# Cross-attention on one NeuronCore: the value products of two head groups run back to back, and the normalized input moves into three shared buffers

## The chip, the cores and the metric

The kernel runs on one core of one Trainium2 chip. The metric is the device time in microseconds. A core has a matrix engine (TensorE: PE for its matmuls, PEld for its weight loads), a vector engine (VectorE, DVE), a scalar engine (ScalarE, ACT), a general one (GpSimd, POOL) and a queue engine (SyncE, SP) that issues nearly every DMA of this kernel. Each engine works through its own instructions in the order in which the program gives them; engines wait for each other by semaphores.

## The reference

Layer normalization, a query projection, attention of 32 heads over a context that serves as keys and values, an output projection and a residual:

```python
x = (hidden - mu) * rsqrt(var + 1e-5) * gamma + beta   # hidden: 8 x 256 x 1024
Q = split_heads(x @ Wq.T)                              # 32 heads of 32
K = V = split_heads(ctx)                               # ctx: 8 x 256 x 1024
probs = softmax(where(mask, Q @ K.T / sqrt(32), -inf))
out = hidden + merge_heads(probs @ V) @ Wout.T         # all float32
```

## The kernel before

**The quad and the slot.** Four heads are 128 columns and make a quad; each of the 8 batches has 8 quads, so there are 64 quads, numbered n. The main loop at L938 has 64 passes; this text calls pass n "slot n". i is n modulo 8, and b in the loop is the batch whose output is projected in that slot (batch n // 8 - 1).

**What a slot puts on PE, in this order** (L963 to L1028): the scores of quad n + 1 (L486, 16 matmuls in the trace), the values of quad n - 2, which is probabilities times V (L636, 64 small matmuls on 64 rows by 32 columns, eight of them side by side in the array), "place 1" steps of the output projection (L720), one of the seven products of a later batch's query projection (L447), and "place 2" steps of the output projection. Both projections are done by Strassen's scheme in Winograd's form, seven half-size products A11, A12, S2, S3, A22, S1, S4 of four steps each; a step shows as two matmuls of 512 columns in the trace. `STEPS` (L669) says how many steps stand in each place of the slots i = 0 to 8 (8 is the next batch's slot 0); `PRODUCTS` gives their order. `ENDS` is the table of the last but one batch. The query product p of a batch falls into slot i = 2 + p.

**The accumulator of the output projection.** Pool `ps_o` has one buffer. The first step of A12, of S2 and of S1 begins a new sum in it, and so PE must wait there until DVE has read the sum before: `store(b, 0, 0)` in slot i = 2 (L762, before S2), `store(b, 1, 0)` in slot i = 6 (before S1), `store(b, 0, 1)` in slot i = 0. A11 has the query projection's buffer `ps_q`, which ACT empties in `keep_p1` (L728).

**What a slot puts on the other engines: `softmax(n + 1)`.** For each of the four heads j: DVE reads the two score tiles, adds the mask and finds the smallest value of the negated scores (L524), ACT takes the exponential and its sum (L528), DVE the reciprocal (L535), POOL multiplies (L543), DVE transposes 32 x 32 blocks into the tile `pT` (L549), and ACT copies a part aside (L555). In between ACT copies the finished values out of PSUM (`copy_at`, L649), DVE takes sums of the output projection (the "hooks") and a query product (`copies`). The next scores need the score buffers that L524 has read. At the end of the slot comes `tail` (L609): SP issues two DMAs that exchange quarters of `pT` (L614), then the loads of the list `between` (L615), then two more for `pT` (L618), each of which waits for its partner of L614 to land.

**The loads.** `between` holds, in this order, the V of the next two quads (odd slots) or a K (even slots), in some slots a half of `ring`, the weights of a query product (slots i = 7 and i = 0 hold the two halves of T1, 512 KB each), a residual (i = 0 to 3), and a half of the x of a later batch (L129, 512 KB).

**The path of x.** For batch b the tables at L816 to L842 give the slot of each step, relative to first = 8 (b - 1) + 2, the slot of its first query product. The two halves s = 0, 1 of x are loaded; DVE takes their statistics (`ln_stats`, L227 to L232, which stand behind the slot's softmax and ahead of the next slot's); ACT normalizes (L248); DVE transposes blocks into a second tile xe (`blocks_x`, L316); 16 DMAs move its blocks into a third tile xnT (`move_x`, L332), from which PE reads. x and xe alternate in two buffers of pool `xp`; xnT has two buffers of pool `lnp`, the first of which held batch 0's xnT.

```python
    loads=(first - 12, first - 11) if b == SPLIT + 1 else (first - 13, first - 12),
    stats=(first - 10, first - 8) if b == SPLIT + 1 else (first - 11, first - 9),
```

For b = 4 to 7 these are, by i: loads 5 and 6, statistics 7 and 1, moves 4, 5 and 6 (of the slots before the batch's first product).

Of the kernel before, what the change touches and what calls it, by code (L numbers as in the profile page):

```python
# [46 lines left out]
F32 = mybir.dt.float32  # L47
# [4 lines left out]
P = 128  # L52
# [7 lines left out]
def xattn_kernel(  # L60
# [15 lines left out]
    NQ = NC  # L76
# [9 lines left out]
    N = B * NQ  # L86

    const = ctx.enter_context(tc.tile_pool(name="const", bufs=1))
    xp = ctx.enter_context(tc.tile_pool(name="xp", bufs=2))
    rp = ctx.enter_context(tc.tile_pool(name="rp", bufs=4))  # L90
    lnp = ctx.enter_context(tc.tile_pool(name="lnp", bufs=2))
    kp = ctx.enter_context(tc.tile_pool(name="kp", bufs=2))
    vp = ctx.enter_context(tc.tile_pool(name="vp", bufs=2))
    atp = ctx.enter_context(tc.tile_pool(name="atp", bufs=3))
# [24 lines left out]
        nc.tensor.transpose(busy, ident, ident)  # L119


    xs, ks, vs, rs = {}, {}, {}, {}

    def load_x(b, s, h=None):

        if b not in xs:
            xs[b] = xp.tile([P, NS, D], F32, tag="x", name=f"x_{b}")
        cols = ds(0, D) if h is None else ts(h, 512)
        nc.sync.dma_start(xs[b][:, s, cols], x[b, ts(s, P), cols])  # L129

# [124 lines left out]
            ALU.subtract, ALU.mult,  # L255
        )

    xnT0 = lnp.tile([P, NC, S + 1], F32, tag="xnT", name="xnT_0")
    xnTs[0] = lambda c: xnT0[:, c, :]
    px0 = {}  # L260

# [36 lines left out]
    def transpose_x1(p):  # L298

        if p == 0:  # L300
            tile_ = lnp.tile([P, NC * (S + 1)], F32, tag="xnT", name="xnT_1")
            px1["to"] = tile_[:, : NC * S].rearrange("p (c t) -> p c t", c=NC)
# [9 lines left out]
    def blocks_x(b, s):  # L312

        if s == 0:
            xes[b] = xp.tile([P, NA, NC, NS, K], F32, tag="x", name=f"xe_{b}")
        nc.vector.transpose(  # L316
            xes[b][:, :, :, s, :],
            xs[b][:, s, :].rearrange("p (c q k) -> p q c k", c=NC, q=NA),
        )

    def move_x(b, part):

        if 0 in part:
            tile_ = lnp.tile([P, NC * (S + 1)], F32, tag="xnT", name=f"xnT_{b}")
            xnT = tile_[:, : NC * S].rearrange(
                "p (a c s k) -> p a c s k", a=NA, c=NC, s=NS
            )
# [167 lines left out]
    tails = []  # L495
    BY_ACT = range(1, 2 * NQ)
    BY_DVE = range(NQ, 2 * NQ)


    def softmax_parts(n, copies=(), ahead=(), between=(), hooks={}, fill=()):  # L500
# [9 lines left out]
                fill.pop(0)()  # L510

        pss = scs[n]
        pT = pTs[n] = ptp.tile([P, 2, NI, NH, NS, K], F32, tag="pT", name=f"pT_{n}")
        pc = asp.tile([P, NI, NH, NS, K], F32, tag="pc", name=f"pc_{n}")
        es, mns, dens = {}, {}, {}

# [40 lines left out]
        if n == 0:  # L557
            for j in range(NH - 1):
                exps(j, (0,))
            yield  # L560
            exps(NH - 1, (0,))
            fill_in()
            yield
            for j in range(NH):
                exps(j, (1,))
            normalize(0)
            fill_in()
        else:
            exps(0)
            while tails:  # L570
                tails.pop()()
            for done in list(pvs):
                copy_at(done)
            exps(1)
            for hook in hooks.get("soon", ()):
                hook()
            exps(2)
            normalize(0)
            exps(3)
        if n <= NQ + 1:  # L580
# [44 lines left out]
            tail()  # L625
        yield

    def values(n):
        pvs[n] = [
            ps_v.tile([P, 2, NS, K], F32, tag="pv", name=f"pv_{n}_{r}") for r in range(2)  # L630
        ]
        pT = pTs.pop(n)
        for i in range(NI):
            for j in range(NH):
                for r in range(2):
                    nc.tensor.matmul(  # L636
                        pvs[n][r][j * HD : (j + 1) * HD],
                        vs[n - n % 2][ts(r, 2 * K), i, ds(n % 2 * P + j * HD, HD)],
                        pT[ts(r, 2 * K), :, i, j, :, :],
                        start=(i == 0), stop=(i == NI - 1),  # L640
                    )

    def copy_at(n):
        b, c = divmod(n, NQ)
        k, c = divmod(c, NK)
        if c == 0:
            ats[b, k] = atp.tile([P, NK, NS, NA, K], F32, tag="at", name=f"at_{b}_{k}")
        for r, pv in enumerate(pvs.pop(n)):
            nc.scalar.copy(  # L649
                ats[b, k][:, c, :, ts(r, 2), :], pv.rearrange("p a s k -> p s a k")  # L650
            )
# [28 lines left out]

# [51 lines left out]

    def copy_po(b, i):
        if "tile" not in ends_kept:
            tile_ = lnp.tile([P, NC * (S + 1)], F32, tag="xnT", name="ends")
            ends_kept["tile"] = tile_[:, : 4 * 512].rearrange("p (i q) -> p i q", i=4)
        ends_kept[i] = ends_kept["tile"][:, i % 4]
        nc.scalar.copy(ends_kept[i], pos[b])

# [198 lines left out]
    for n in range(N):  # L938
# [17 lines left out]
        if n in (2, 4):  # L956
            between.append(partial(load_wo, B21, n // 2 - 1))
        if n == N - 4:
            again = xp.tile([P, NS, D], F32, tag="x", name="x_again")
# [203 lines left out]
```

## Time and profile before

| | |
|---|---|
| Time, median of 3 runs (lowest to highest) | 567.86 us (567.67 to 568.67) |
| Span of the profiled execution, first to last instruction | 566.0 us |
| Median time less that span | 1.9 us |
| Granted TensorE clock, mean | 1.000 |
| Busy share of PE, DVE, ACT, POOL | 99%, 83%, 75%, 70% |
| DMA | 119.02 MB in 47219 packets, mean 210 GB/s |

The profile is of one execution; the time of that execution itself is known by its span. The span runs from the first to the last instruction of the program, and the time has 1.9 us more than that around it. In the chain of waits every piece begins where the instruction of that piece is started and ends where the next piece begins, so the pieces of one engine add up without overlap. In the lists of instructions by time, a row is a run of one kind: its start, its length until the last one ends, and its count.

### The profile page before, as it was taken

To read this page: it belongs to the slowest core of one execution; us is meant where nothing else is said; L and a number is where in the kernel's file an instruction comes from. 1 tells how busy PE (TensorE), PEld (TensorE's weight loads), DVE (VectorE), ACT (ScalarE), POOL (GpSimd) and SP (SyncE) were. 2 spreads that over 40 slices of the span, in tenths; PEclk is the share of its full clock that TensorE was granted. 3 is DMA by queue.
4 is the path that set the end of the run, shared out by engine and by line. 5 is a ranking of instruction groups with operands and counts; after the bars stand their busy time and mean duration, and the time that the engine had idled before them with its cause. 6 is when DMAs were issued, how large, how long until landed. Compare 5 with 4: busy or idle time off the path is not lost.

```text
span 566.0 us, 20200 instructions
## 1 busy us (share of the span) xinstructions
PE 561.4 (99%) x7266; PEld 393.7 (70%) x7266; DVE 467.6 (83%) x1716; ACT 423.4 (75%) x1464; POOL 394.3 (70%) x636
## 2 busy tenths in 40 slices
PE   8999999999999999999999999999999999999997
PEld 8788886767766767667766776667766767755454
DVE  5889889999988988878898888988888777879923
ACT  4699999997778866786777876778776776769820
POOL 2788887899777656857568665777648657448780
PEclk9999999999999999999999999999999999999999
DMA  8966667856697777966778767796658864536751
GB/s 310 397 181 199 185 198 228 281 162 179 212 301 232 223 202 235 263 195 191 233 216 239 215 176 221 230 273 193 176 140 269 255 191 128 146 110 180 218 156 74
DMA packets 47219, 119.02 MB, mean 210 GB/s; under 512 B 8976, under 2 KB 9744, under 8 KB 47120
## 3 DMA queue, kind: packets, MB, share of 16 engines
q1 hardware_dynamic: 46976, 117.74, 69.5%
q8 instruction: 57, 0.93, 0.8%
q14 instruction: 42, 0.34, 0.2%
q10 hardware_dynamic: 144, 0.01, 0.0%
HBM read 66.33 MB, written 11.53 MB: 138 GB/s over the span
## 4 chain that ended last, share of the span: by engine, by line
PE 97%; DMA 1%; DVE 0%; POOL 0%; ACT 0%; issue 0%; SPq 0%; POOLq 0%
PE po_S L720 21%; PE pq_A L447 19%; PE pv L636 12%; PE sc L486 12%; PE po_A L720 11%; PE pq L345 9%; PE pq_S L447 8%; PE po_end L787 3%; PE po_last L787 1%; DMA x<-in_x_dram 1%; PE po_end_s L787 0%; POOL x L885 0%; PE pq L290 0%; PE px L307 0%; ACT e L528 0%; PE px L273 0%
## 5 line engine op out<-in xcount | busy, mean ns | idle before, releaser
L543 POOL TENSOR_SCALAR e<-e,rden 128x256 f32<-128x256 f32 x466 | 215.4, 479 | 125.5 <-DVE rden L535 123.0
L528 ACT ACTIVATE e<-e,mn 128x256 f32<-128x256 f32 x512 | 254.0, 502 | 46.1 <-DVE mn L524 44.9
L549 DVE STREAM_TRANSPOSE pT<-e 128x512 f32<-128x512 f32 x256 | 178.9, 703 | 35.6 <-POOL e L543 27.5
L524 DVE CUSTOM_DVE_ANT_0 e<-sc,mb 128x256 f32<-128x256 f32 x512 | 185.3, 415 | 25.4 <-PE sc L486 25.1
L555 ACT COPY pc<-pT 128x512 f32<-128x512 f32 x128 | 79.0, 617 | 55.7 <-DVE pT L549 35.6
L528 ACT ACTIVATION_READ_ACCUMULATOR e<-e,mn 128x1 f32 x512 | 98.4, 192 | 0.0
L486 PEld LDWEIGHTS sc<-k,qa 32*128 32x128 f32 x1024 | 46.1, 184 | 42.2 <-issue 21.6
L720 PE MATMUL po_S<-wo,at 128*128 128x512 f32 x152 | 74.3, 606 | 0.0
L636 PE MATMUL pv<-pT,v 64*32 64x128 f32 x4096 | 74.1, 274 | 0.0
L486 PE MATMUL sc<-k,qa 32*128 32x256 f32 x1024 | 73.6, 401 | 0.1
L636 PEld LDWEIGHTS pv<-pT,v 64*32 64x32 f32 x4096 | 57.0, 105 | 22.5 <-issue 11.8
L720 PE MATMUL po_A<-wo,at 128*128 128x512 f32 x128 | 59.4, 605 | 0.0
L345 PE MATMUL pq<-xnT,wq 128*128 128x256 f32 (+1 forms) x240 | 55.0, 384 | 0.0
L447 PEld LDWEIGHTS pq_A<-xnT,wq 128*128 128x128 f32 x416 | 48.5, 192 | 6.2 <-issue 4.8
L345 PEld LDWEIGHTS pq<-xnT,wq 128*128 128x128 f32 x240 | 44.6, 190 | 8.2 <-issue 1.5
L720 PE MATMUL po_S<-wo,s 128*128 128x512 f32 x104 | 50.1, 606 | 0.0
L447 PE MATMUL pq_A<-xnT,wq 128*128 128x128 f32 x416 | 48.5, 275 | 0.0
L535 DVE RECIPROCAL rden<-den 128x2 f32<-128x2 f32 x256 | 38.2, 150 | 7.3 <-ACT e L528 6.2
L524 DVE DVE_READ_ACCUMULATOR2_ANT mn<- 128x1 f32 x512 | 42.4, 83 | 0.0
L720 PEld LDWEIGHTS po_A<-wo,at 128*128 128x128 f32 x128 | 22.9, 189 | 25.6 <-issue 24.5
L720 PEld LDWEIGHTS po_S<-wo,at 128*128 128x128 f32 x152 | 25.5, 190 | 19.5 <-issue 19.5
L753 POOL TENSOR_TENSOR r<-r,p 128x512 f32<-128x512 f32 x24 | 30.6, 1277 | 4.8 <-ACT e L528 3.0
(102 smaller groups left out, 666.1 us busy)
## 6 DMA issues: line engine op xcount, KB each, us to landing
v<-in_kv_dram SPq DMA_DIRECT2D x32, 512.0 KB, 4.2
pT<-pT SPq DMA_DIRECT2D x128, 128.0 KB, 2.9
pT<-pc SPq DMA_DIRECT2D x128, 128.0 KB, 4.0
ring<-kept_T SPq DMA_DIRECT2D x20, 512.0 KB, 5.3
k<-in_kv_dram SPq DMA_DIRECT2D x32, 256.0 KB, 4.1
x<-in_x_dram SPq DMA_DIRECT2D x15, 512.0 KB, 5.6
r<-in_x_dram SPq DMA_DIRECT2D x28, 256.0 KB, 4.5
out_dram<-r SPq DMA_DIRECT2D x28, 256.0 KB, 3.2
```

The lines of the kernel that those rows point to most:

```text
L345: nc.tensor.matmul(pqs[n], wq[:, o, c, :], xnTs[b](c), start=(c == 0), stop=(c == NC - 1),)
L447: nc.tensor.matmul(pqs[b][:, o, :], w[:, c], x_[:, c], start=begins and o + c == 0, stop=c == NK - 1, skip_group_check=True,)
L486: nc.tensor.matmul(scs[n][j][:, s, :], qa[r, n % NQ, ts(s, P)], ks[n - n % 2][r, n % 2, :], start=True, stop=True,)
L524: nc.vector.tensor_tensor_reduce(out=e[:, s, :], in0=pss[j][:, s, :], in1=mbs[n // NQ], scale=1.0, scalar=NO_SCORE, op0=ALU.add, op1=ALU.m ...
L528: nc.scalar.activation(e[:, s, :], e[:, s, :], AF.Exp, bias=mn[:, s : s + 1], scale=-1.0, accum_out=den[:, s : s + 1],)
L535: nc.vector.reciprocal(rden, dens[j])
L543: engine.tensor_scalar(es[j][:, s, :], es[j][:, s, :], rden[:, s : s + 1], 1.0, ALU.mult, ALU.mult,)
L549: nc.vector.transpose(pT[:, :, :, j, :, :].rearrange("p a i s k -> p (a i) s k"), es[j].rearrange("p s (b t) -> p b s t", t=K),)
L555: nc.scalar.copy(pc[:, :, ts(j, 2)], pT[:, 1, :, ts(j, 2)])
L636: nc.tensor.matmul(pvs[n][r][j * HD : (j + 1) * HD], vs[n - n % 2][ts(r, 2 * K), i, ds(n % 2 * P + j * HD, HD)], pT[ts(r, 2 * K), :, i, j, ...
L720: nc.tensor.matmul(po, operand(b, name)[:, c], wo[:, which, c], start=begins and c == 0, stop=c == NK - 1, skip_group_check=not begins,)
L753: nc.gpsimd.tensor_tensor(r, r, p1s[b], ALU.add)
```

## The change

Three things change.

1. In slots 16 to 55 (`PAIRED`) the values are done in odd slots only, for two quads in one run: slot n does quads n - 3 and n - 2, in the two halves of the same two PSUM tiles. `copy_at` of both stands behind the third head's exponentials instead of behind the first's. The output projection of batches 1 to 5 gets a step table of its own, `PAIR_STEPS`.
2. Probabilities live longer, so a fourth `pT` is needed. Every fourth quad's `pT` (n % 4 == 3, from quad 11 on) has a fixed tile `first_or_pT`, which at first holds batch 0's xnT.
3. The pools `xp` and `lnp` go. Three fixed tiles, `rooms`, hold x, xe and xnT of all later batches: x and xnT of batch b share room b - 1, xe has room b (modulo 3). The loads of x move from first - 13 and first - 12 to first - 11 and first - 10 (batch 3: from first - 12 and first - 11 to first - 10 and first - 9), and the first half's statistics from first - 11 to first - 10 (batch 3: first - 10 to first - 9). For b = 4 to 7 that is, by i: loads 7 and 0, statistics 0 and 1.

```diff
-    xp = ctx.enter_context(tc.tile_pool(name="xp", bufs=2))
-    lnp = ctx.enter_context(tc.tile_pool(name="lnp", bufs=2))
+    first_or_pT = const.tile([P, NC * (S + 1)], F32, tag="first", name="first_or_pT")
+    rooms = [const.tile([P, NC * S], F32, tag=f"room{i}", name=f"room_{i}") for i in range(3)]
+    def room(which, shape, **sizes):
+        return rooms[which % 3].rearrange(shape, **sizes)
...
-            xs[b] = xp.tile([P, NS, D], F32, tag="x", name=f"x_{b}")
+            xs[b] = room({0: 1, 1: 2}.get(b, b - 1), "p (s d) -> p s d", s=NS)
...
-            xes[b] = xp.tile([P, NA, NC, NS, K], F32, tag="x", name=f"xe_{b}")
+            xes[b] = room(b, "p (a c s k) -> p a c s k", a=NA, c=NC, s=NS)
...
+            xnT = room(b - 1, "p (a c s k) -> p a c s k", a=NA, c=NC, s=NS)
...
+    PAIRED = range(2 * NQ, N - NQ)
...
+        if n >= NQ and n % 4 == 3:
+            pT = first_or_pT[:, : NC * S].rearrange(
+                "p (a i j s k) -> p a i j s k", a=2, i=NI, j=NH, s=NS
+            )
+        else:
+            pT = ptp.tile([P, 2, NI, NH, NS, K], F32, tag="pT", name=f"pT_{n}")
...
             exps(0)
             while tails:
                 tails.pop()()
-            for done in list(pvs):
-                copy_at(done)
+            if n - 1 not in PAIRED:
+                copy_ats()
             exps(1)
             for hook in hooks.get("soon", ()):
                 hook()
             exps(2)
+            if n - 1 in PAIRED:
+                copy_ats()
             normalize(0)
...
-    def values(n):
-        pvs[n] = [
-            ps_v.tile([P, 2, NS, K], F32, tag="pv", name=f"pv_{n}_{r}") for r in range(2)
+    def values(n, also=()):
+        both = [
+            ps_v.tile([P, 1 + len(also), 2, NS, K], F32, tag="pv", name=f"pv_{n}_{r}")
+            for r in range(2)
         ]
+        for u, one in enumerate((n, *also)):
+            pvs[one] = [pv[:, u] for pv in both]
+            one_quad(one)
...
     STEPS = ((0, 0, 0), (0, 7, 0), (0, 1, 2), (0, 2, 2), (0, 2, 1), (0, 1, 2), (0, 0, 3), (0, 1, 2),
              (0, 2, 0))
+    PAIR_STEPS = ((0, 0, 0), (0, 6, 0), (0, 2, 3), (0, 1, 1), (0, 3, 2), (0, 0, 2), (0, 0, 4),
+                  (0, 0, 1), (0, 3, 0))
...
-        return STEPS
+        return PAIR_STEPS if NQ * (b + 1) in PAIRED else STEPS
...
-                loads=(first - 12, first - 11) if b == SPLIT + 1 else (first - 13, first - 12),
-                stats=(first - 10, first - 8) if b == SPLIT + 1 else (first - 11, first - 9),
+                loads=(first - 10, first - 9) if b == SPLIT + 1 else (first - 11, first - 10),
+                stats=(first - 9, first - 8) if b == SPLIT + 1 else (first - 10, first - 9),
...
-        if n >= 2:
+        if n not in PAIRED and n >= 2:
             values(n - 2)
+        elif n in PAIRED and n % 2:
+            values(n - 3, (n - 2,))
```

More of the change, by code (lines that the diff above doesn't have):

```diff
@@ L256, in ln_norm @@
         )
-    xnT0 = lnp.tile([P, NC, S + 1], F32, tag="xnT", name="xnT_0")
+    xnT0 = first_or_pT.rearrange("p (c t) -> p c t", c=NC)
     xnTs[0] = lambda c: xnT0[:, c, :]
@@ L300, in transpose_x1 @@
         if p == 0:
-            tile_ = lnp.tile([P, NC * (S + 1)], F32, tag="xnT", name="xnT_1")
-            px1["to"] = tile_[:, : NC * S].rearrange("p (c t) -> p c t", c=NC)
+            px1["to"] = room(0, "p (c t) -> p c t", c=NC)
             xnTs[1] = lambda c: px1["to"][:, c, :]
@@ L323, in move_x @@
         if 0 in part:
[L324 to L327, printed above, removed]
+            xnT = room(b - 1, "p (a c s k) -> p a c s k", a=NA, c=NC, s=NS)
             to_move[b] = xnT
@@ L512, in softmax_parts @@
         pss = scs[n]
-        pT = pTs[n] = ptp.tile([P, 2, NI, NH, NS, K], F32, tag="pT", name=f"pT_{n}")
+        if n >= NQ and n % 4 == 3:
[4 more added lines that the diff above has]
+            pT = ptp.tile([P, 2, NI, NH, NS, K], F32, tag="pT", name=f"pT_{n}")
+        pTs[n] = pT
         pc = asp.tile([P, NI, NH, NS, K], F32, tag="pc", name=f"pc_{n}")
@@ L626, in softmax_parts, with one_quad @@
         yield
-    def values(n):
-        pvs[n] = [
-            ps_v.tile([P, 2, NS, K], F32, tag="pv", name=f"pv_{n}_{r}") for r in range(2)
-        ]
+    def values(n, also=()):
+        both = [
+            ps_v.tile([P, 1 + len(also), 2, NS, K], F32, tag="pv", name=f"pv_{n}_{r}")
+            for r in range(2)
+        ]
+        for u, one in enumerate((n, *also)):
+            pvs[one] = [pv[:, u] for pv in both]
+            one_quad(one)
+    def one_quad(n):
         pT = pTs.pop(n)
@@ L641, in values, with copy_ats @@
                     )
+    def copy_ats():
+        for done in list(pvs):
+            copy_at(done)
     def copy_at(n):
@@ L734, in copy_po @@
         if "tile" not in ends_kept:
-            tile_ = lnp.tile([P, NC * (S + 1)], F32, tag="xnT", name="ends")
-            ends_kept["tile"] = tile_[:, : 4 * 512].rearrange("p (i q) -> p i q", i=4)
+            ends_kept["tile"] = room(B - 1, "p (i q) -> p i q", i=4)
         ends_kept[i] = ends_kept["tile"][:, i % 4]
@@ L958, in xattn_kernel @@
         if n == N - 4:
-            again = xp.tile([P, NS, D], F32, tag="x", name="x_again")
+            again = room(B, "p (s d) -> p s d", s=NS)
             for s in range(NS):
```

## The prediction

> **What bounds the kernel now.** First the page: busy shares, then the chain of waits.
>
> ```profile
> span 566.0 us, 20200 instructions
> PE 561.4 (99%) x7266; PEld 393.7 (70%) x7266; DVE 467.6 (83%) x1716; ACT 423.4 (75%) x1464; POOL 394.3 (70%) x636
> ...
> PE 97%; DMA 1%; DVE 0%; POOL 0%; ACT 0%; issue 0%; SPq 0%; POOLq 0%
> ```
>
> The chain is 97% PE, and every piece of it in the middle is a matmul run, so PE's queue alone sets the end. A busy PE need not be a gapless one, so I took the chain piece by piece over slots 31 to 34 (columns: start, us until the next piece, what).
>
> ```profile
> 276.22 1.08 PE sc L486 x16
> ...
> 284.73 1.08 PE sc L486 x16
> 285.81 1.09 PE pv L636 x64
> 286.89 1.91 PE po_S L720 x4
> 288.81 3.57 PE pq_A L447 x32
> 292.38 1.08 PE sc L486 x16
> 293.45 1.09 PE pv L636 x64
> 294.54 6.21 PE po_A L720 x14
> 300.75 1.08 PE sc L486 x16
> 301.82 1.09 PE pv L636 x64
> 302.91 1.05 PE po_A L720 x2
> 303.96 3.57 PE pq_S L447 x32
> 307.54 1.72 PE po_S L720 x4
> 309.25 1.08 PE sc L486 x16
> ```
>
> Slot 31 (i = 7) lasts 284.73 - 276.22 = 8.51 us, slot 32 (i = 0) 7.65, slot 33 (i = 1) 8.37, slot 34 (i = 2) 8.50. A step of the output projection is 0.86 (two of 1.72 / 4). After values the same four matmuls take 1.91, not 1.72: 0.19 for coming out of the small-matmul form. PE waits for nobody here, so the question is twofold: how much PE work goes, and whether someone is now late for PE.
>
> **PE's part.** Is the 0.19, and the 0.30 at the end of a scores run, paid as well where no values stand between? Slot 0 has scores straight ahead of full-size matmuls:
>
> ```profile
> 22.59 1.08 PE sc L486 x16
> 23.67 3.67 PE pq L345 x16
> ```
>
> Scores cost 1.08 there too, and the entry cost shows again, so an even slot loses one values run of 1.09 and nothing else. The odd slot gets a second quad without a new entry. Its price is not in the trace, as no run is longer than 64. The nearest row is the second half of a run that begins at 251.77 on the chain's clock and 251.70 by the list:
>
> ```profile
> 252.16 0.70 PE L636 MATMUL pv<-pT,v 64*32 64x128 f32 x32
> ```
>
> The last 32 start within 0.70 less one matmul's 0.27, or 0.43, and the first 32 took 252.16 - 251.70 = 0.46. So 64 more cost 2 x 0.44 = 0.88; the bounds are 0.86 (twice 0.43) and 1.09 (a run that starts afresh). Gain per pair 1.09 - 0.88 = 0.21, bounds 0.23 and 0. Slots 17 to 55 hold 20 pairs: **-4.2 us**, bounds -4.6 and 0.
>
> The step table only moves steps (28 before and after). New slot lengths: i = 7 (three steps to one, second quad) 8.51 - 1.72 + 0.88 = 7.67; i = 0: 7.65 + 0.86 - 1.09 = 7.42; i = 1: 8.37 - 0.86 + 0.88 = 8.39; i = 2: 8.50 + 1.72 - 1.09 = 9.13.
>
> [...]
>
> **What hides, and under what.** The copies out of PSUM move behind the third head and come four at a time, twice the two below, in odd slots alone: +0.30 on ACT there, -0.30 in even ones. The slack that covers it: DVE has read its last scores about 4.2 us into a slot (2.81 after its first read, below), and PE wants those buffers at 8.4. Without that cover it would cost 0.3 a pair, 6 us. `pT` may be late as well: the odd quad's values stand in the same slot as before, the even quad's one slot later, and each tile is overwritten no sooner after its reading than before. Rooms and views issue no instructions. In slot i = 6 the S1 product comes sooner: 1.08 + 3.67 = 4.75 after the slot's start, while DVE's `store` before it ends about 3.5 after its first read at 1.1, or 4.6. It fits; if by a hair it does not, 0.1 x 5.
>
> **The load of x and its statistics, on the path.** This is the part that I think decides. The statistics stand in DVE's queue between the last block of a slot and the first scores of the next, so if x has not landed, everything of DVE behind them waits: the exponentials, the sums of the output projection, and behind those PE. Before, two to three slots lay between a load and its statistics; now one. The load is issued in the slot's `tail`, which waits for the slot's last copy aside; so "one slot later" is one slot less the tail's delay. DVE and ACT in slots 31 to 34 (columns of these and the next rows: start, us, engine, line, what):
>
> ```profile
> 293.03 0.70 DVE L549 STREAM_TRANSPOSE pT<-e 128x512 f32<-128x512 f32 x1
> 293.65 0.39 DVE L524 CUSTOM_DVE_ANT_0 e<-sc,mb 128x256 f32<-128x256 f32 x1
> ...
> 299.90 0.71 DVE L549 STREAM_TRANSPOSE pT<-e 128x512 f32<-128x512 f32 x1 [0.27 <-POOL e L543]
> 300.53 1.25 DVE L227 BATCH_NORM_STATS2 st<-x 128x6 f32<-128x512 f32 x2
> 302.13 0.41 DVE L524 CUSTOM_DVE_ANT_0 e<-sc,mb 128x256 f32<-128x256 f32 x1
> ...
> 304.94 0.69 DVE L762 TENSOR_TENSOR r<-po_A,r 128x512 f32<-128x512 f32 x1
> 284.68 0.62 ACT L555 COPY pc<-pT 128x512 f32<-128x512 f32 x1 [0.41 <-DVE pT L549]
> 295.28 0.40 ACT L649 COPY at<-pv 128x128 f32<-128x128 f32 x2
> ```
>
> To be seen: slot 32's last block ends 293.73, 9.0 after the slot's start; in slot 33 the last block ends 6.96 after the first read (300.61 - 293.65); statistics hold DVE for 1.52 (300.61 to 302.13); the store that frees the accumulator ends 3.50 after the slot's first read (305.63 - 302.13). And the queue's issues, then the landings of DMAs (last column: us from issue; the two x loads are those of batches 6 and 7 before the change):
>
> ```profile
> 286.50 1.72 SPq L614 DMA_DIRECT2D pT<-pT  x2
> 288.27 0.57 SPq L143 DMA_DIRECT2D v<-in_kv_dram  x1
> 288.89 0.45 SPq L412 DMA_DIRECT2D ring<-kept_T  x1
> 294.40 1.78 SPq L614 DMA_DIRECT2D pT<-pT  x2
> 297.35 0.43 SPq L149 DMA_DIRECT2D r<-in_x_dram  x1
> v<-in_kv_dram SPq DMA_DIRECT2D x1, 512.0 KB, 3.9
> ring<-kept_T SPq DMA_DIRECT2D x1, 512.0 KB, 5.2
> r<-in_x_dram SPq DMA_DIRECT2D x1, 256.0 KB, 5.4
> x<-in_x_dram SPq DMA_DIRECT2D x1, 512.0 KB, 5.5
> x<-in_x_dram SPq DMA_DIRECT2D x1, 512.0 KB, 7.3
> ```
>
> In slot 31 the tail begins at 286.50, V lands at 292.17 and the ring half at 294.09: 7.6 after the tail's start, 1.9 after V. In the new order x stands behind that ring half, so another 1.9: 9.5 after the tail's start. The tail can start when ACT's copy ends, 285.30 or 9.1 into the slot, plus 0.3 for the extra copies; before, the queue was late (10.3) through the moves and the x loads of slots 29 and 30, the latter now gone. I take 9.5.
>
> First half: 9.5 + 9.5 = 19.0 into slot i = 7, which is 19.0 - 7.67 = 11.3 into slot i = 0. DVE is free at 9.0, so it waits 2.3, ends the statistics at 12.8, and begins slot i = 1's reads 12.8 - 7.42 = 5.4 into it (1.3 before). They end at 8.25, just ahead of PE's next scores at 8.39. The last block ends at 5.4 + 6.96 = 12.4.
>
> Second half: slot 32's tail began 9.67 into the slot (294.40), and the residual, the last before x, landed at 302.75, 8.35 later; x another 1.9: 19.9 into slot i = 0, 12.5 into slot i = 1. Statistics end at 14.0, so slot i = 2's reads begin 14.0 - 8.39 = 5.6 into it, and the store ends at 9.1. PE wants the first S2 step at 1.08 + 1.91 + 3.57 = 6.56 (6.79 before, with DVE done at 4.9). **PE stands 2.5 us.** The wait lengthens slot i = 2 to 11.7, in which DVE catches up, so nothing is carried on.
>
> Bounds of that stall: with x always in time, 9.0 + 1.52 - 7.42 = 3.1, + 6.96 + 1.52 - 8.39 = 3.2, + 3.5 = 6.7: 0.15. At the worst (tail at 10.3 as before, x issued 3 later and taking 7.3) the first statistics end 7.0 into slot i = 1, PE's scores wait 1.45 there and S2 2.6 more: 4.05. I take 2.5: the ring and residual ahead of x are certain, and their rows agree.
>
> Batches 4 to 7 have it, at slots 16 to 42: 4 x 2.5 = 10.2 (unrounded 2.54). Batch 3's loads and first statistics also move by a slot or two, at slots 8 to 10, but its second statistics stay where they were: estimate 1.1, bounds 0 and 2.6. Together **+11.3**, bounds 0.6 and 18.8.
>
> **Sum.** 566.0 - 4.2 + 11.3 = 573.1 of span, and 1.9 around it as before: 575.0 against the median 567.86.
>
> **The rivals.**
>
> A, the other side: the loads are in time. Then 566.0 - 4.2 + 0.6 + 1.9 = 564.3, faster. For it: single x loads land 5.5 after issue, and fewer loads crowd slots i = 5 and 6. It decides at the landing of the second half: the total breaks even at about 1 us a batch, which is x 10.9 into slot i = 1, 8.7 after the tail's start. Against it: the residual alone landed 8.35 after, and x follows it. 22%.
>
> B, worse: the queue is as late in slot i = 7 as it was, so PE's next scores wait too: 566.0 - 4.2 + 18.8 + 1.9 = 582.5. For it: the sixteen moves still stand right ahead. Against it: two x loads fewer among them. 20%.
>
> C, the pairs gain nothing, because a run slows past 64: at a second price of 1.09 the time is 575.0 + 4.2 = 579.2, and the change does not do what it is built to do. Against it: 0.43 for the second half of the run. 6%. [...]
>
> D, stalls and gain cancel within the measurement: 567.9, 4%.
>
> **Chances.** The forecast has 48%, its own range 570 to 580. This kernel's measurement tells 0.2%, 1.1 us, from no change. Faster is A, 0.22; same is D, 0.05 with the rims of its neighbours; slower is the forecast, B and C, 0.73. The range takes in A's value and most of B: 563.5 to 581.
>
> **What would show it.** The pairs: runs x128 of 1.97 us in the chain, gaining 0.2 each. The loads: DVE idle ahead of L227 with the x load as releaser, some 2 us in slots i = 0; first reads some 5 us into slots 17, 18, 25, 26, 33, 34, 41 and 42; gaps on PE before the S2 matmuls of slots 18, 26, 34 and 42, put down to DVE L762. The prediction is wrong if x lands before the slot's last block, or if PE's S2 steps follow the query product without a gap.

## The result, and the profile after

| | before | after |
|---|---|---|
| Time, median of 6 runs each on one chip (lowest to highest) | 567.93 us (567.67 to 569.4) | 597.39 us (595.94 to 600.95) |
| Ratio, with its 95% interval | | 1.0517 [1.0494, 1.054] |
| Span of the profiled execution | 566.0 us | 595.5 us |
| Granted TensorE clock, mean | 1.000 | 0.983 |

The change makes the kernel slower by 5.2%. The direction was forecast; the size, 29.5 us instead of 7, lies outside the range. Ratios leave out executions more than 1.5% above the fastest of the same kernel (three of the six of e12 below, one of the six of e13). First the page of the changed kernel: the span, the busy shares, and the shares of the chain of waits.

```profile
span 595.5 us, 20172 instructions
PE 574.8 (97%) x7266; PEld 402.6 (68%) x7266; DVE 464.4 (78%) x1716; ACT 423.7 (71%) x1464; POOL 394.9 (66%) x636
...
PE 74%; DVE 8%; DMA 5%; ACT 5%; POOL 4%; issue 3%; SPq 1%; DVEq 0%; POOLq 0%; ACTq 0%
```

The number of matmuls is the same, and the chain that was 97% PE is now 74%. PE is busy for 13.4 us more with the same work (574.8 against 561.4): a first sign that some of it ran at a lower clock. The chain of waits around slot 34 (start, us until the next piece, what; the last two rows are of slot 35):

```profile
321.27 1.18 DVE st L231 x2
...
325.68 0.61 DVE r L782
326.34 4.54 PE po_S L741 x6
...
331.95 2.08 PE pv L651 x127
334.03 0.83 issue
```

The chain now leads from the statistics of x over DVE's reads to the store, and only then to PE's S2 matmuls. The list of PE's instructions by time shows the idle time itself, in brackets, for slot 34:

```profile
316.37 1.80 PE L486 MATMUL sc<-k,qa 32*128 32x256 f32 x16
...
326.34 4.54 PE L741 MATMUL po_S<-wo,s 128*128 128x512 f32 x6 [2.67 <-DVE r L782]
```

Six matmuls of S2 hold PE for 4.54 us, where six take 2.84 at full clock (in a run shown below). The windows of the same kernel (stretch, its length, PE's busy time with its instructions, and so on; the granted clock stands behind POOL's) say why:

```profile
300.00:308.00 8.00, 8.00 (x60) 5.63 (x60) 6.74 (x27) 6.13 (x22) 4.12 (x10) 1.00 0.65 180
...
326.30:330.30 4.00, 3.96 (x6) 1.62 (x6) 2.89 (x7) 3.02 (x11) 3.85 (x8) 0.57 1.06 308
...
326.89:330.30 3.41, 3.41 (x6) 1.30 (x4) 2.30 (x6) 2.43 (x8) 3.41 (x8) 0.50 1.07 294
```

PE's clock averaged 0.57 in the four microseconds after the wait: it was 0.50 from 326.89 to 330.30, and 1.00 on either side. So this wait of 2.67 us cost another 1.7 (4.54 less 2.84) once it was over, half of those 3.41 us.

Not every wait did this. In this trace the granted clock stands at 1.00 or at 0.50, and its changes (169.87, 180.11, 241.55, 244.97, 326.89, 330.30, 401.98 and 405.39) lie 0, 3, 21, 22, 46, 47, 68 and 69 steps of 3.41 us from the first of them. Counted by such intervals, it is PE's idle time between two steps that goes with the change. The traces before and after have 304 intervals between 12 and 545 us that began at 1.00: four had 2.66 to 2.95 us of idle time and were followed by 0.50, and the 300 others, with 1.36 us at most, were followed by 1.00. Over the traces of all 16 kernels, all 22 with 2.0 us or more were followed by 0.50, and of the 2420 others three (0.6 to 1.7 us idle). The wait of slot 34 fell into one interval. That of slot 10, 2.48 us, was cut into 1.11 and 1.37, and the clock stayed at 1.00:

```profile
106.39 1.98 PE L741 MATMUL po_S<-wo,s 128*128 128x512 f32 x4 [2.48 <-DVE r L782]
```

The longest wait after which the clock stayed at 1.00 was 3.16 us, in slot 35 of the run e2 below; it was cut into 1.44 and 1.72, and the 32 matmuls of the query product soon behind it took 3.57 us, as at full clock:

```profile
326.16 1.12 PE L741 MATMUL po_S<-wo,s 128*128 128x512 f32 x2 [3.16 <-issue]
```

In all, the changed kernel ran at 0.50 for 20.5 us (10.24 from 169.87, and 3.41 each from 241.55, 326.89 and 401.98), which is worth 10.2 us of PE's work at most.

The worst place is slots 16 to 18, batch 4. The chain there:

```profile
160.17 8.48 DMA room<-in_x_dram
...
168.67 1.30 DVE st L231 x2
...
171.13 4.20 PE sc L486 x16
...
179.04 4.14 PE pq_S L447 x32
```

The x load takes 8.48 us, DVE stands until it lands, and PE's scores of slot 18 wait for DVE; then the clock is 0.50 from 169.87 to 180.11. The scores, which also go at the pace of DVE's reads, take 4.20 us and the product 4.14, for what takes 1.08 and 3.57. DVE's waits over the whole run, in one row (us in total, times, longest):

```profile
DVE st L231 <- DMA room<-in_x_dram: 25.6, 9, 8.2
```

And slot 25 shows something else. Its chain:

```profile
236.77 2.00 PE pv L651 x120
238.77 2.67 issue
241.44 0.57 PE pv L651 x4
242.01 6.83 PE po_A L741 x12
```

PE stops four matmuls before the end of a pair run for 2.67 us, waiting for nothing that the profile shows as a semaphore; after it the twelve matmuls of the projection take 6.83 us, where they take 5.35 in an undisturbed run (shown below); the clock was 0.50 from 241.55 to 244.96. The DMA view of 239.04 to 240.17 has one packet of a queue, q8, that moved nothing from 224.95 to 239.0:

```profile
q8 instruction: 1, 0.02, 6.2%
```

Queue q8 moved 57 packets of 16 KB in the run. That they bring PE's instructions, 256 to a packet, is an estimate from counts of this trace. It has 14532 matmuls and weight loads and 214 instructions of PE's sequencer, 14746 together, and 57 x 256 = 14592 agrees to about 1%; and each of the 57 packets, k counted from 0, begins to move when PE has started 154 to 449 instructions more than 256 k. The 449 belongs to the packet of slot 25, at 239.04, with PE already at a stand. The last one before had landed at 224.9, and this one lands at 240.16; PE goes on 1.3 us after that. Slots 35 (0.83, the last row of the first chain) and 47 stop in the same way.

**Slot by slot.** The start of each slot is the start of its scores. Against the slots of before, and for kernels with pair runs against the length that an undisturbed pair pattern gives (taken from the quietest slots: i = 0 to 7 differ by -0.23, +0.09, +0.63, -0.77, +0.63, +0.09, -0.15, -0.77 us), the changed kernel loses 2.74 us in slot 10, 4.28 and 5.42 in slots 17 and 18, 4.69 in 25, 5.30 in 34, 0.95 in 35, 6.27 in 42, 1.08 in 47. That is 30.7, with 1.1 scattered; the pairs bring -2.4; by slot 61 it is 29.45 behind.

### The profile page after: what moved, and what is told of

It reads as the page before. It is cut to its first block, busy times and chain, and to the rows that moved or that the text cites. A ratio compares the mean times of both kernels' runs of the same rounds, so it can differ in the third digit from the quotient of the medians.

```text
span 595.5 us, 20172 instructions
## 1 busy us (share of the span) xinstructions
PE 574.8 (97%) x7266; PEld 402.6 (68%) x7266; DVE 464.4 (78%) x1716; ACT 423.7 (71%) x1464; POOL 394.9 (66%) x636
## 4 chain that ended last, share of the span: by engine, by line
PE 74%; DVE 8%; DMA 5%; ACT 5%; POOL 4%; issue 3%; SPq 1%; DVEq 0%; POOLq 0%; ACTq 0%
PE po_S L741 20%; PE pq_A L447 19%; PE sc L486 9%; PE pv L651 9%; PE po_A L741 6%; PE pq_S L447 5%; ACT e L535 3%; DMA room<-in_x_dram 3%; DVE e L531 3%; PE po_end L807 3%; POOL e L550 2%; DMA ring<-kept_T 2%; DVE pT L556 2%; DVE st L231 1%; PE po_last L807 1%
## 5 line engine op out<-in xcount | busy, mean ns | idle before, releaser
L556 DVE STREAM_TRANSPOSE pT<-e 128x512 f32<-128x512 f32 x200 | 139.6, 703 | 32.2 <-POOL e L550 29.3
L562 ACT COPY pc<-pT 128x512 f32<-128x512 f32 x100 | 61.6, 617 | 37.8 <-DVE pT L556 24.2
L486 PE MATMUL sc<-k,qa 32*128 32x256 f32 x1024 | 79.0, 406 | 4.4 <-DVE mn L531 4.2
L651 PE MATMUL pv<-pT,v 64*32 64x128 f32 x3200 | 56.5, 273 | 0.7 <-issue 0.7
L651 PEld LDWEIGHTS pv<-pT,v 64*32 64x32 f32 x3200 | 45.4, 105 | 15.2 <-issue 8.7
L447 PEld LDWEIGHTS pq_A<-room,wq 128*128 128x128 f32 x416 | 48.1, 192 | 4.8 <-issue 3.4
L447 PE MATMUL pq_A<-room,wq 128*128 128x128 f32 x416 | 49.1, 276 | 0.0
L556 DVE STREAM_TRANSPOSE first_or_pT<-e 128x512 f32<-128x512 f32 x56 | 39.1, 702 | 8.2 <-POOL e L550 8.0
L231 DVE BATCH_NORM_STATS2 st<-room 128x6 f32<-128x512 f32 x32 | 20.6, 678 | 25.6 <-DMA room<-in_x_dram 25.6
L741 PEld LDWEIGHTS po_S<-wo,s 128*128 128x128 f32 x104 | 19.3, 200 | 27.8 <-issue 19.2
```

What stands on the lines that cost most here:

```text
L231: nc.vector.bn_stats(sts[b, s][:, h, :], xs[b][:, s, ts(h, 512)])
L447: nc.tensor.matmul(pqs[b][:, o, :], w[:, c], x_[:, c], start=begins and o + c == 0, stop=c == NK - 1, skip_group_check=True,)
L486: nc.tensor.matmul(scs[n][j][:, s, :], qa[r, n % NQ, ts(s, P)], ks[n - n % 2][r, n % 2, :], start=True, stop=True,)
L556: nc.vector.transpose(pT[:, :, :, j, :, :].rearrange("p a i s k -> p (a i) s k"), es[j].rearrange("p s (b t) -> p b s t", t=K),)
L562: nc.scalar.copy(pc[:, :, ts(j, 2)], pT[:, 1, :, ts(j, 2)])
L651: nc.tensor.matmul(pvs[n][r][j * HD : (j + 1) * HD], vs[n - n % 2][ts(r, 2 * K), i, ds(n % 2 * P + j * HD, HD)], pT[ts(r, 2 * K), :, i, j, ...
```

## The experiments

Two theories at first. **Loads**: the short way from load to statistics makes DVE wait, and PE behind it. **Pairs**: the pair runs themselves cost something. A third came from slot 25, **packets**: a pair run uses up 256 instructions in 1.84 us, and the next packet of instructions is not there in time.

The losses of every run by slot, worked out as above (us; "start" is what had been lost by slot 8; losses under 0.35 are left out). Each row is of one execution, the profiled one; in e3, e4 and e5 it was the slowest of four (596.25, 595.77 and 580.81 us against medians of 592.89, 591.85 and 575.6), so the rows tell where a kernel loses and not its median.

| run | span | start | 10, 11 | 17, 18 | 25, 26 | 33, 34 | 35 | 41, 42 | others |
|---|---|---|---|---|---|---|---|---|---|
| after | 595.5 | 0.2 | 2.7 | 9.7 | 4.7 | 5.3 | 1.0 | 6.3 | 47: 1.1 |
| e1 other statistics | 578.6 | 0.8 | 0 | 4.8 | 5.3 | 0.4 | 1.6 | 0 | 47: 1.3 |
| e2 statistics later | 580.5 | 0.5 | 3.2 | 2.5 | 5.6 | 0 | 3.2 | 0 | 47: 1.3 |
| e3 rooms alone | 594.4 | 0 | 3.3 | 7.7 | 6.2 | 6.0 | 0 | 5.2 | |
| e4 loads alone | 594.0 | 0 | 5.2 | 9.1 | 6.2 | 2.9 | 0 | 4.6 | |
| e5 later blocks | 579.0 | 1.7 | 2.8 | 6.3 | 0 | 2.5 | 0 | 0 | 23: 1.3 |
| e6 rooms, loads in time | 569.2 | 0.2 | 0 | 2.3 | 0 | 0 | 0 | 0 | |
| e8 pairs split | 589.0 | 0.3 | 6.0 | 2.5 | 4.2 | 2.5 | 1.2 | 4.1 | 47: 1.2; 50: 1.2 |
| e9 all in time | 573.1 | 1.4 | 0 | 2.8 | 0 | 0.9 | 0 | 0.4 | 23: 1.0; 28: 0.8; 37: 0.4; 47: 0.8 |
| e10 rooms, residual first | 570.5 | 0 | 0 | 4.3 | 0 | 0 | 0 | 0 | |
| e11 pairs, residual first | 573.0 | 2.0 | 0 | 6.8 | 0 | 0 | 0 | 0 | |
| e12 the same, 32 transposes | 576.2 | 0.7 | 0 | 7.0 | 0 | 1.3 | 0.4 | 0 | 37: 1.3; 47: 1.8 |
| e13 T1 early, pairs | 590.0 | 13.2 | 0 | 8.7 | 0.4 | 0.5 | 0 | 0 | 49: 3.1 |
| e14 T1 early, 16 transposes | 582.2 | 1.6 | 0 | 10.8 | 0 | 2.0 | 0 | 0 | 45: 3.7 |
| e15 T1 early, rooms | 574.2 | 0 | 0 | 8.0 | 0 | 0 | 0 | 0 | |

### The loads and the rooms, each alone

Rooms without pairs is the changed kernel with

```diff
-    PAIRED = range(2 * NQ, N - NQ)
+    PAIRED = range(0)
```

> The changed kernel without the pairing: values in every slot, copies early, the old step table; rooms, fourth pT and the later loads and statistics stay. Theory: the waits for x stay and the pairs' gain and the stops inside long values runs go: 583 to 593 us. Rival 1 (pairs are the loss): 568. Rival 2 (rooms): 590 and more, as the theory; told apart by the next run.

Measured: 592.89 us, ratio 1.0437 [1.04, 1.0474]. The loads alone is the kernel before, with its four buffers, and only

```diff
-                loads=(first - 12, first - 11) if b == SPLIT + 1 else (first - 13, first - 12),
-                stats=(first - 10, first - 8) if b == SPLIT + 1 else (first - 11, first - 9),
+                loads=(first - 10, first - 9) if b == SPLIT + 1 else (first - 11, first - 10),
+                stats=(first - 9, first - 8) if b == SPLIT + 1 else (first - 10, first - 9),
```

> The kernel before with nothing but the changed kernel's slots for the loads of x and the statistics; old pools, no pairs. Theory: as the run with rooms alone, within 2 us of it, 583 to 593 us. Rival 2 (the rooms' own dependencies make DMAs or DVE wait): about 568, with the loss only where the rooms are. Rival 1: 568.

Measured: 591.85 us, ratio 1.0417 [1.0365, 1.047]. DVE's waits of this kernel:

```profile
DVE st L227 <- DMA x<-in_x_dram: 25.8, 8, 8.0
```

25.8 us of waiting, with no room and no pair in the kernel, against 25.6 in the changed one. The two agree within their intervals, at the upper end of what was expected. So about four fifths of the loss (23.6 of 29.5 us, by the medians) come with two lines of a table.

### Statistics that need not wait

In the changed kernel the statistics of batches 3 to 7 are taken of a tile that has long been there, so the later values of those batches are not the reference's; the number of instructions is the same.

```diff
-                nc.vector.bn_stats(sts[b, s][:, h, :], xs[b][:, s, ts(h, 512)])
+                nc.vector.bn_stats(sts[b, s][:, h, :], xs[b][:, s, ts(h, 512)] if b < 3 else wo[:, B21, h, :])
```

> The changed kernel, but the statistics of batches 3 to 7 are taken from a resident weight tile instead of x (so the result for these batches is normalized by wrong numbers); every instruction, load and transfer stays. Theory (DVE stands for x, and PE for DVE): the losses of slots 10, 17, 18, 34 and 42, 24 us together in the trace of the changed kernel, go; 566 to 574 us, the upper end if the stops inside the values runs stay. Rival 1 (the paired runs themselves and their late copies are the loss): no lower than 590. Rival 2 (rooms and traffic): no lower than 590.

Measured: 578.98 us, ratio 1.0168 [1.0108, 1.0227], above the expectation. Slots 10, 17, 34 and 42 lose next to nothing now; slot 18 still loses 4.8. But slot 25 still stops, and longer:

```profile
229.56 2.00 PE pv L651 x120
231.56 3.22 issue
```

It stops behind the same matmul as in the changed kernel, 124 of 128, and the packet lands 1.3 us before PE goes on (233.49). This could not have come from x.

The statistics one slot later, with x itself, for batches 4 to 7:

```diff
-                stats=(first - 9, first - 8) if b == SPLIT + 1 else (first - 10, first - 9),
+                stats=(first - 9, first - 8) if b == SPLIT + 1 else (first - 9, first - 8),
```

> The changed kernel with the first half's statistics of batches 4 to 7 one slot later and the second half's too (slots i = 1 and 2 instead of 0 and 1), loads where they are. Theory: x has landed by then (it lands 3.3 to 5.6 us into slot i = 1, DVE comes to the statistics some 8 us into it), so only batch 3's 2.7 us and the stops in the values runs stay: 568 to 577 us. Rivals 1 and 2: 590 or more, as neither pairs nor traffic change.

Measured: 583.33 us, ratio 1.0268 [1.0199, 1.0338]. Slots 34 and 42 lose nothing; slots 25 and 35 stop (3.71 and 3.16 us). And slot 18 has another chain:

```profile
160.68 8.00 DMA room<-in_x_dram
...
168.69 5.53 DMA r<-in_x_dram
...
174.36 1.27 POOL r L773
...
175.66 0.70 DVE r L782
...
176.40 2.84 PE po_S L741 x6
```

The residual's load is issued at the moment when x has landed, though it needs neither its tile nor its data. It is the eighth transfer behind it in SP's order. Over all of SP's 552 transfers of the changed kernel, a late issue (0.3 us or more behind the one before) falls within 0.06 us of the landing of the second to seventh transfer before it 33 times, where most are the `pT` moves that wait for their partner; of the eighth before it 15 times, 14.4 us together; of the ninth to sixteenth never. In the kernel before it is 15 times too. The trace of the changed kernel also has the reason: SP's transfers take eight semaphores in turn (541 of 544 use that of the eighth transfer before them), and the issue of the residual in slot 18, at 168.67, waits for semaphore 109, which the load of x (issued at 160.17, landed at 168.65) raises; SP stood 2.06 us for it. So it was a semaphore of the program by which the slow transfer held the whole queue, eight further on.

### Are the stops packets of instructions?

Counting PE's instructions in the trace (matmuls, weight loads and the sequencer's), a pair run begins at some number past a multiple of 256. In the changed kernel and the two experiments above, the runs that stop are those that begin at 199, 192 and 201 (slots 25, 35, 47). Of the others none loses over 0.3; the nearest begin at 162 and 234. And the place where PE stops is each time 193 past a multiple (PE goes on there at 241.44, 334.87 and 444.46 in the changed kernel), whether that falls into the run, or, as for the one that begins at 192, just behind it. If that is the cause, shifting every number moves the stops to other slots. The kernel with later statistics, and half the warm-up:

```diff
-    for _ in range(32):
+    for _ in range(16):
         nc.tensor.transpose(busy, ident, ident)
```

> The statistics of batches 4 to 7 one slot later, as in the experiment with later statistics (583.33 us), and 16 of the 32 warm-up transposes at the very start left out, so that every later PE instruction has a number lower by 32. Theory (instruction packets): PE stops in a pair run when a packet of 256 instructions is fetched as the run begins; the runs of slots 25, 35 and 47 begin 192 to 201 past a multiple of 256. With 32 fewer they begin at 160 to 169, like the runs of slots 37 and 49 before, which did not stop: slots 25, 35 and 47 lose their stops (8.7 us together, all but some 0.5), and the run of slot 45, which now begins at 202, stops instead, by 1 to 5 us; slot 23 (209) may stop. Time 575 to 580. Rival (the place decides: the transfers or the PSUM of these slots): the stops stay in slots 25, 35 and 47 with the same lengths, and the time stays at 583.

Measured: 575.6 us, ratio 1.0138 [1.0089, 1.0187]. The chain at slots 23 and 25:

```profile
219.59 1.99 PE pv L651 x117
221.58 0.96 issue
...
236.09 2.03 PE pv L651 x124
238.13 5.35 PE po_A L741 x12
```

Slots 25, 35 and 47 run through, and slot 23, which now begins at 209, stops. Slot 45 (202) was expected to stop and lost only 0.2: its packet landed 0.3 us after the run's start, that of slot 23 1.8 after. The transfers themselves took 1.20 us (slot 23) and 0.89 (slot 45), but one began 0.6 us after the run's start and the other 0.6 ahead of it. So in these runs the place in the packet told which runs could stop, and the moment at which the packet landed which of them did.

### A step of the projection between the two quads

Later statistics again, and

```diff
-            values(n - 3, (n - 2,))
+            values(n - 3, (n - 2,), now=False)
+            one_quad(n - 3)
         project_steps(n, 1)
+        if n in PAIRED and n % 2:
+            one_quad(n - 2)
```

> Statistics of batches 4 to 7 one slot later, as in the experiment with 583.33 us, and in odd slots the projection steps of place 1 between the two quads of values instead of behind them. Theory (a run of 256 PE instructions in 1.84 us is too dense for the packets): no stops in slots 25, 35 and 47 (8.7 us gone), and each pair pays again for leaving and entering the small form (0.2 each, 3 to 4 us in all): 577 to 580. Rival (something else stops PE there): the stops stay, 586 to 588.

Measured: 590.26 us, ratio 1.0368 [1.0337, 1.0398], the wrong way and above both expectations: the second quad's values end up to six steps (5.35 us) later, ACT's copies wait for them, and slots 26, 34 and 42 lose 2.5 to 4.2 us. (Slot 10 has no pair; its loss comes from batch 3's statistics, as in e2.) For the packets it tells something all the same. Its chain in slots 25, 35 and 47:

```profile
233.15 1.09 PE pv L652 x64
234.24 5.35 PE po_A L742 x12
...
327.80 1.07 PE pv L652 x62
328.87 0.47 issue
...
433.57 2.00 PE pv L652 x119
435.57 0.85 issue
```

With six steps in between, slot 25 does not stop (2.67 to 3.71 us in the runs above). With one step, slot 35 stops for 0.47. Slot 47 (i = 7) has no step in place 1, so there the run is as dense as before, and it stops for 0.85.

### Everything in time

All of batches 3 to 7: loads in first - 10 and first - 9, statistics in first - 8 and first - 7, every later step one slot later, the 16 moves eight to a slot.

```diff
+                loads=(first - 10, first - 9),
+                stats=(first - 8, first - 7),
+                norms=(first - 7, first - 6), trans=(first - 6, first - 5),
+                moves=tuple(first - 5 + i // 8 for i in range(16)),
```

Without pairs:

> The rooms without pair runs, and for all batches from 3 on the loads in first - 10 and first - 9, statistics in first - 8 and first - 7, each later step one slot later too, the 16 moves in two slots instead of three. Theory (only the time between load and statistics costs): no DVE wait for x, no loss in slots 10, 17, 18, 26, 34, 42; 567 to 570. Rival (sharing three rooms costs in itself, or a residual behind x does): 574 to 590, with the losses still in slot 18 and 26.

Measured: 570.14 us, ratio 1.0032 [1.0013, 1.005]. The rooms cost nothing but slot 18, where the second reason was right: a residual, issued when a T1 half lands.

```profile
159.63 5.75 DMA ring<-kept_T
...
165.39 6.48 DMA r<-in_x_dram
...
173.30 0.70 DVE r L782
...
174.05 1.98 PE po_S L741 x4
```

With pairs, and 22 warm-up transposes:

> Pair runs and rooms, with the loads and statistics as in the run of this call without pairs, and 22 warm-up transposes instead of 32, so that no pair run begins between 182 and 213 past a multiple of 256. Theory: nothing waits for x and no packet stops a run: 562 to 566, faster than both kernels by what the pairs save (0.1 to 0.2 each). If packets still stop runs that begin at 172 to 181 or 214 to 221: 566 to 573. Rival (the pairs bring nothing even without stops): the same time as the run without pairs.

Measured: 575.03 us, ratio 1.011 [1.0092, 1.0129]. No DVE wait for x is left. That is above every expectation. It is 4.9 us slower than without pairs, so the pairs do not pay even here. Slots 34 and 42 lose to residuals again, perhaps since the shorter slots give a load less time, which was not tested; slot 23 (begins at 221) and slot 47 (178) stop; the shorter warm-up loses 1.4 by slot 8.

### The residual first

```diff
-                between.append(partial(load_res, b, *((0, 0), (0, 1), (1, 1), (1, 0))[i]))
+                between.insert(n % 2, partial(load_res, b, *((0, 0), (0, 1), (1, 1), (1, 0))[i]))
```

> The rooms without pair runs, loads and statistics as in the run with 570.14 us, and each residual issued ahead of its slot's K (behind V in odd slots) instead of behind K, V and ring. Theory (the 2.3 us left in slot 18 were the residual, which POOL and then DVE's store wait for): slot 18 at 8.5 to 9.3 us instead of 10.84, 567.5 to 569, the same as before. Rival (the rooms cost something there): slot 18 stays at 10.8, 570.

Measured: 573.28 us, ratio 1.0077 [1.0055, 1.01]; slot 18 at 12.85 us. Neither theory. The residual is no longer late, but the second T1 half has become the eighth behind the first:

```profile
159.53 6.26 DMA ring<-kept_T
...
165.80 6.44 DMA ring<-kept_T
...
172.29 3.17 PE pq_S L447 x16
```

The wait only changed its owner.

> Pair runs with all loads in time, residuals first, and 16 warm-up transposes (pair runs begin at 160 to 169 and 202 to 209 past a multiple of 256). Theory: the pairs save 0.12 each by the slots' lengths (2.4 us for 20), one run (slot 23) stops for 1.2, the shorter warm-up costs about 1.1 at the start: span 565.5 to 567.5, time 567 to 569.5, the same as before within the measurement. Rival (pairs save 0.21 each as predicted): 565 to 566. Other rival (pairs bring further waits of their own): 571 or more.

Measured: 575.61 us, ratio 1.0141 [1.0122, 1.016]. The other rival by its number, but not by its reason: outside slot 18 (6.8) and the start (2.0) no slot loses over 0.21, and no run stops.

> The same with all 32 warm-up transposes, so the pair runs of slots 25, 35 and 47 begin at 192 to 201 past a multiple of 256 again. Theory: these three stop PE, 3 to 8 us together, with nothing else late: 570 to 575, in spite of the longer warm-up. Rival (the stops came from late loads or a slow clock and not from the packets): the same time as the run with 16, or 1 us less.

Measured: 573.03 to 583.72 us, ratio 1.0139 [1.0106, 1.0171]; the profiled span is 576.2, against 573.0 with 16. In time the two cannot be told apart. In the trace slots 35, 37 and 47 (190, 160, 198) lose 3.4 us, where with 16 transposes they lose 0.2; slot 25 (198) runs through, its packet landing 0.2 us after the run's start. In slot 37, whose run begins at 160, PE stops not in the run but 16 matmuls of the product later, which is again 193 past a multiple:

```profile
336.25 2.04 PE pv L651 x119
338.29 1.98 PE pq_A L447 x16
340.27 1.00 issue
```

Slot 34 loses its 1.3 to a T1 half, the eighth behind the other.

### The T1 halves of batch 3 earlier

With residuals first and loads in time, the T1 halves of batch 3 in slots 14 and 15 instead of 15 and 16, one of them ahead of V. Three kernels.

> Pair runs, loads in time, residuals first, the T1 halves of batch 3 in slots 14 and 15 instead of 15 and 16; the warm-up has 26 full and 26 small transposes, so pair runs begin 40 later than in the changed kernel: at 231 to 241 in slots 25, 35 and 47, and at 197 to 200 in slots 37 and 49. Theory: slot 18 loses nothing, the pairs save 2.4, slots 37 and 49 stop for 1 to 3 us together: 566.5 to 569. If they do not stop: 566. Rival (slot 18 has another cause): 570 or more, with slot 18 at 11 us or more.

Measured: 594.99 us, ratio 1.0438 [1.0402, 1.0475]. 13.2 us of it are the start: full and small transposes in turn take 0.65 us a pair, and the warm-up 16.9 us instead of 5.8, so PE was not ready for the first x. Slot 18 lost 8.7, so the theory failed there too. Slot 37 ran through; slot 49, which begins at 195, stopped:

```profile
449.57 2.05 PE pv L652 x125
451.62 2.74 issue
```

> The same with 16 full warm-up transposes and none small (runs begin at 158 to 169, and at 199 to 209 in slots 23 and 45). Theory: slot 18 loses nothing, the start costs 1.1 to 1.9, stops 0 to 1.3: 567 to 569.5. Rival as in the other: 571 or more.

Measured: 584.84 us, ratio 1.0273 [1.0236, 1.031]. Slot 18 loses 10.8, and slot 45 (begins at 199) stops for 1.7 us and loses 3.7, with the clock at 0.50 from 414.26 to 417.68.

> The same without pair runs and with all 32 warm-up transposes. Theory (the rooms cost nothing once every load is in time): span 566 to 566.5, the same time as before, 568. Rival (the rooms cost something of their own in slot 18): 570 or more.

Measured: 576.85 us, ratio 1.014 [1.0122, 1.0158]. Slot 18 loses 8.0. The move was a mistake: SP now waits until 147.97 for the ring with the T1 half of slot 14, the exchanges of `pT` behind it are late (issued at 148.38 and 161.40, where e6 has 146.12 and 157.74), and PE's values wait for them.

```profile
161.40 3.19 DMA pT<-pT
...
164.66 7.41 DMA pT<-pc
...
172.16 2.33 PE pv L651 x64
```

No version was found that beats the kernel before; the nearest is the rooms with all loads in time, at 1.0032.

## Why the prediction was right in direction and too small

**PE bound, gapless.** Right.

**The pairs, -4.2.** Mis-sized. The chain has 2.04 us for a whole pair run and had 1.09 for one quad, so the second quad costs 0.95 and not 0.88; by the slots' lengths a pair saves 0.12, 20 pairs 2.4. That lies inside the bounds (0 and 4.6). The slowing past 64 of rival C was a small one: in runs of 128, 127 steps in 1.84 us are 14 ns each. New slot lengths were forecast as 7.67, 7.42, 8.39 and 9.13; undisturbed ones are 7.74, 7.42, 8.46 and 9.14.

**What hides.** Right for the late copies, the rooms and `pT`: with everything in time (e9, e11) nothing in i = 3 to 7 waits for them. The edit's cost in instruction packets was not thought of at all: a pair run was priced as PE time alone. It is 4.69 + 0.95 + 1.08 = 6.7 us of the loss (1.5 of it the low clock behind slot 25), and shown by moving the stops with the numbers (e5, e13, e14).

**The load of x, +11.3.** This is the step that failed: the term measured 24.0 (2.7 for batch 3, 21.3 for batches 4 to 7). The mechanism was right, step by step, for batch 6, slots 32 to 34 (starts 300.46, 307.88, 316.37). First half: landed at 312.43, 12.0 into slot 32 (forecast 11.3); DVE waited 3.16 (2.3). Second half: landed at 320.55, 12.7 into slot 33 (12.5). The store ended at 326.29, 9.9 into slot 34 (9.1). PE stood 2.67 (2.5). What was mis-sized is what PE pays for it:

- The clock. The sum let PE go on at full speed. In slot 34 six matmuls took 1.7 longer, at 0.50 of the clock for 3.41 us. The length of the wait alone did not decide it: 2.67 us was enough here, and 3.16 us in slot 35 of e2 was not. What went with it was the idle time between two of the steps of 3.41 us, 2.67 us in slot 34 and 1.44 and 1.72 in e2.
- The scores. They were forecast to be ready 0.14 ahead of PE; they were late, and the 16 matmuls of slot 34 took 1.80 instead of 1.15. With the wait, the clock, and 0.26 for starting anew after a wait (six matmuls in 2.84 instead of 2.58), 0.65 + 2.67 + 1.70 + 0.26 make 5.28 of the 5.30.
- So 5.3 and 6.3 us in slots 34 and 42, where 2.5 stood, and where the bound of 4.05 was meant to be the worst.
- Batch 4, 9.7 in slots 17 and 18. The DMA engines were busier there (98% from 158 to 172 us, 86% from 303 to 317 for batch 6): x took 8.48, and the ring half and the residual behind it were held by the eighth transfer before them; then the clock was at 0.50 for 10.24 us. The forecast took all batches to be alike.
- Batch 5 lost nothing of this kind in slot 26, behind the stop of slot 25; e3 and e4, which have no stops, lose 6.2 there.
- Batch 3, 2.74 where 1.1 stood (bounds 0 and 2.6).

By terms: forecast -4.2 + 1.1 + 10.2 + 0; measured -2.4 + 2.7 + 21.3 (9.7 + 0 + 5.3 + 6.3) + 6.7, which is 28.3 of the 29.45.

**The rivals.** A (loads in time) fell by e4; even where it holds, in e6 and e9, the time was not under the one before. B named the right place, the scores of slots 17 and 18, for one batch of four. That the sum with its 18.8 was "the worst" was the mistake: bounds of the wait alone were no bounds of the loss, as the clock fell after it (5.3 us in slot 34 for a wait of 2.67).

**Still open.** What sets the moment at which a packet's transfer begins, and so whether a run in danger stops; and why the clock fell after three intervals with little idle time (0.6, 0.9 and 1.7 us). And slot 18: with everything else in time it loses 2.3 to 10.8, and each order of the queue that was tried moved the wait to another transfer.

## What to carry to other kernels

A load that moves nearer to its use should be priced by its place in the queue, and by all that is issued behind it; and a wait of the busiest engine by what it costs afterwards too (here 1.7 us, half of 3.41 at the low clock, behind 2.67). An engine that is fed by small instructions has a second supply to watch, that of the instructions themselves: here a run of 256 in 1.84 us could outrun it. When one wait is taken out of a full queue, look at which transfer becomes the late one before counting the gain.

## What the runs showed of the hardware that was not expected

- PE ran out of instructions, by the estimate of 256 to a packet of 16 KB. A dense run stopped PE at 193 past a multiple of 256, for 0.5 us in slot 35 of e8 and up to 3.7 in slot 25 of e2. In the changed kernel PE went on 1.3 us after a packet had landed (240.16, 333.61 and 443.19; PE at 241.44, 334.87 and 444.46). The runs that stopped within themselves or just behind began at 190 to 221 past a multiple, but not all that began there stopped (slot 45 of e5, at 202, and slot 25 of e12, at 198, ran through); one at 178 (e9) and one at 160 (e12) stopped 7 and 16 matmuls behind their ends.
- PE's clock was halved three times for 3.41 us, and once for 10.24, each time after an interval of 3.41 us in which PE had been idle for 2.66 to 2.95 us. Where a wait fell counted beside its length: 2.67 us in slot 34 did it (0.50 from 326.89 to 330.30); 2.48 in slot 10, cut in two by a step, did not: granted 1.00 from 106.4 to 110.0, just behind it.
- Small matmuls in a run of 128 started 14 ns apart (127 steps in 1.84 us), as in a run of 64; full and small transposes in turn took 0.65 us a pair (e13), against 0.18 for a full one alone (32 in 5.8 us).
- The residual's load of slot 18 waited for the eighth transfer before it by a semaphore that the program uses for both: 109, raised when x had landed at 168.65, and the residual issued at 168.67. Whether the queue would have taken it sooner with another semaphore was not tested.
